# Gated cross-attention in fp32: a setup with fewer, larger DMAs on one queue, block transposes on VectorE, and W_mem's product with chunks outermost

## The chip, the cores and the metric

The kernel runs on one NeuronCore of a Trainium2 chip. The metric is device time in microseconds (us); a profiled execution of the same program gives the trace. Engines are TensorE (PE, with its weight load PEld), VectorE (DVE), ScalarE (ACT), GpSimd (POOL) and SyncE (SP, which here only issues DMAs).

## The reference

`x` is 8 x 1024 x 1024, `memory` (ctx_1024) is 8 x 64 x 512, all in float32.

```python
memory_proj = einsum('bme,de->bmd', memory, W_mem)              # d = 1024, e = 512
scores = einsum('bnd,bmd->bnm', x, memory_proj) / sqrt(1024)
attn = softmax(scores, axis=-1)
memory_context = einsum('bnm,bmd->bnd', attn, memory_proj)
gate = sigmoid(einsum('bnf,df->bnd', concat([x, memory_context]), W_gate) + b_gate)
fused = x + gate * memory_context
return fused * rsqrt(mean(fused**2, -1) + 1e-6) * norm_w
```

## The kernel before, in words

**The main loop.** The rows of x are taken in 16 steps of 512. A step's product of x with the first half of W_gate is a two-level fast matrix product (seven outer products, `outer_product`, each of seven inner ones named kA to kF, where A is used twice); its left operands are sums of x blocks made on VectorE (`outer_s`) and GpSimd (`inner_s`), its right operands are sums of weight blocks, made once in the setup. Scores, softmax and the two small products with the memory's rows (`pc` is the context, the others add the gate's share) are placed between them by slot numbers: `plan(q)` writes down at which slot or beside which product each piece runs. There are 49 slots in a step.

**x and its transposes.** `load_xq` brings 128 rows in as four DMAs, one for each group of 32 partitions, cut so that VectorE's transpose of 32x32 blocks (`transpose_x`) gives the transposed operand `a`. The chunks of the feature axis come out in an order in which a chunk takes 32 columns from each quarter; weights are loaded in the same order (`rows_by_chunk`). `xqpool` has four buffers of 4 KB per partition, so a step's x fills all four.

**The setup.** This is where the change lies. In order:

- `mem` (512 rows of all batches) is loaded in four pieces of 128 rows. TensorE transposes it against an identity (line 165, tiles `pt_mem`), and VectorE copies the result to `memT` (line 171).
- `wm`, W_mem transposed, comes as four chunks of 128 rows; VectorE reorders each to `wmp` (line 179).
- `pm`: for each of the eight output chunks j, the four chunks k of the contraction are accumulated in one PSUM bank. ScalarE and VectorE copy the banks in turn to `mpT` (lines 201 and 203), and pairs of chunks are stored to a DRAM scratch tensor `mpd`, from which a batch's part is read back later as `mpb`.
- `pt_mp`: TensorE transposes mp back into rows (line 211), ScalarE copies it out (line 213), and it is stored to the DRAM scratch `mgd`.
- `pg`: memory rows times the second half of W_gate (`w2`, tiles `w`), in eight banks: four for the first half of the columns and four for the second. The first half of w2's columns is loaded at the start, the second only after the first bank, since the seven buffers of `gpool` hold four. VectorE adds the bias (tile `g`, line 93), and `g` goes to `mgd` too.
- Between pg's banks VectorE works through `w1_tasks`: four outer and 28 inner sums over W_gate's first half, in the tiles `ws` (outer sums 128x2048, inner 128x512). After the seventh bank come the transposes and sums of the first x step (`first`), and GpSimd's `inner_s`.

**Queues.** Loads go through SyncE's queue (`load`), the stores of mpd and mgd through ScalarE's (`scratch`). `pin` keeps program order on each engine and queue. Completion is tracked by eight semaphores, given out in program order over both queues: a DMA is issued only once the one that last had its semaphore has landed. Nearly all matmuls have line 90, tensor operations on two operands line 93, and SyncE's DMAs line 96, as these are helpers.

The waits between engines follow from the tiles: a tile of a pool can be written again only when all readers of its earlier use are done. `mpT` shares its buffers with the left operands `l` of the main loop (tag "l2"), and in the setup pg reads it to the end.

Of the kernel before, what the change touches and what calls it, by code (L numbers as in the profile page):

```python
# [8 lines left out]
F32 = mybir.dt.float32  # L9
# [6 lines left out]
P = 128  # L16
# [4 lines left out]
def tile_gated_cross_attention_rmsnorm(  # L21
# [57 lines left out]
    xqpool = ctx.enter_context(tc.tile_pool(name="xqpool", bufs=4))  # L79
# [15 lines left out]
    def load(o, i):  # L95
        pin(nc.sync.dma_start(o, i))

    def scratch(o, i):
        pin(nc.scalar.dma_start(o, i))

    def t4k(pool, shape, tag, name):
        return pool.tile(shape, F32, tag=tag, name=name)

    def rows_by_chunk(w):

        return w.rearrange("(i j r) f -> i r j f", i=4, r=32)
# [3 lines left out]
    def bank(n, shape, name):  # L110
        return ps.tile(shape, F32, tag=banks[n % 5], name=name)


    memr = mem.rearrange("b m e -> (b m) e").rearrange("(q p) e -> p q e", p=P)
    mem_sb = [t4k(rot, [P, 2, E], "l2", f"mem_sb{i}") for i in range(2)]
    for q in range(NPAIR):
        load(mem_sb[q // 2][:, q % 2, :], memr[:, q, :])
    wm = []
    for k in range(KE):
        t = t4k(xqpool, [P, D], "xq", f"wm{k}")  # L120
        load(t, w_mem_t[k * P : (k + 1) * P, :])
        wm.append(t)
    bias_sb = t4k(small, [P, D], "junk", "bias_sb")
    load(bias_sb, b_gate.partition_broadcast(P))
    w2r = rows_by_chunk(w_gate_t[D:, :])
    w2 = {}

    def load_w2(h):
        for k in range(KD // 2):
            t = t4k(gpool, [P, 2, H], "gate", f"w2_{k}_{h}")  # L130
            for i in range(4):
                load(
                    t[32 * i : 32 * (i + 1), :, :],
                    w2r[i][:, 2 * k : 2 * k + 2, h * H : (h + 1) * H],
                )
            w2[k, h] = t

    load_w2(0)

    w1r = rows_by_chunk(w_gate_t[:D, :])  # L140
    ws = {o: const.tile([P, 7, 2, C], F32, name=f"ws{o}") for o in range(1, 8)}
    R11, R21, R12, R22, T4, T1, T2 = range(7)
    for o, k, h in ((1, 0, 0), (7, 0, 1), (3, 1, 1), (2, 1, 0)):
        for i in range(4):
            for n in range(2):
                load(
                    ws[o][32 * i : 32 * (i + 1), 2 * n : 2 * n + 2, :, :],
                    w1r[i][:, 4 * k : 4 * k + 4, h * H + n * C : h * H + (n + 1) * C],
                )
# [9 lines left out]
    mgd = dram.tile([B, 2, M, D], F32, name="mgd")  # L159
    memT = [t4k(apool, [P, 2, BM], f"a1{i + 1}", f"memT{i}") for i in range(2)]  # L160
    for q in range(NPAIR):
        pt = bank(q, [P, KE, P], f"pt_mem{q}")
        for k in range(KE):
            pin(
                nc.tensor.transpose(
                    pt[:, k, :], mem_sb[q // 2][:, q % 2, k * P : (k + 1) * P], ident
                )
            )
        for i in range(2):
            pin(  # L170
                nc.vector.tensor_copy(
                    memT[i][:, :, q * P : (q + 1) * P], pt[:, 2 * i : 2 * i + 2, :]
                )
            )
    wmp = []
    for k, tag in enumerate(("a21", "a22", "s1", "s2")):
        t = t4k(apool, [P, KD, P], tag, f"wmp{k}")
        pin(
            nc.vector.tensor_copy(
                t.rearrange("p j (i r) -> p j i r", r=32),  # L180
                wm[k].rearrange("p (i j r) -> p j i r", i=4, r=32),
            )
        )
        wmp.append(t)

# [6 lines left out]
    def mp_rows(j, q):  # L192
        return mpT[j // 2][:, j % 2, q * P : (q + 1) * P]

    for j in range(KD):
        pm = bank(j, [P, BM], f"pm{j}")
        for k in range(KE):
            mm(pm, wmp[k][:, j, :], memT[k // 2][:, k % 2, :], k == 0, k == KE - 1)
        dst = mpT[j // 2][:, j % 2, :]
        if j % 2 == 0:  # L200
            pin(nc.scalar.copy(dst, pm))
        else:
            pin(nc.vector.tensor_copy(dst, pm))
            scratch(mpd[:, j - 1 : j + 1, :], mpT[j // 2])

    for q in range(NPAIR):
        stage = t4k(xqpool, [P, D], "xq", f"mp{q}")
        for h in range(2):
            pt = bank(2 * q + h, [P, 4, P], f"pt_mp{q}_{h}")
            for j in range(4):  # L210
                pin(nc.tensor.transpose(pt[:, j, :], mp_rows(4 * h + j, q), ident))
            pin(
                nc.scalar.copy(
                    stage.rearrange("p (i j r) -> p j i r", i=4, r=32)[
                        :, 4 * h : 4 * h + 4, :, :
                    ],
                    pt.rearrange("p j (i r) -> p j i r", r=32),
                )
            )
        for i in range(2):  # L220
            scratch(mgd[2 * q + i, 0], stage[i * M : (i + 1) * M, :])


    def outer_sum(o, a, b):
        tt(nc.vector, ws[o][:, 0:4, :, :], ws[a][:, 0:4, :, :], ws[b][:, 0:4, :, :], ALU.subtract)

    def inner_sums(o):
        w = ws[o]
        for s, a, b in ((T1, R12, R11), (T2, R22, T1), (R12, R22, R12), (T4, R21, T2)):
            yield lambda s=s, a=a, b=b: tt(  # L230
                nc.vector, w[:, s, :, :], w[:, a, :, :], w[:, b, :, :], ALU.subtract
            )
# [6 lines left out]
        lambda: outer_sum(7, 3, 7),  # L239
        lambda: outer_sum(4, 2, 6),  # L240
    ] + [f for o in (6, 7, 5, 4, 2, 3) for f in inner_sums(o)]
# [9 lines left out]
    def load_xq(q, t):  # L251
        b, n0 = where(q, t)
        xq[q, t] = tl = t4k(xqpool, [P, 4, Q4], "xq", f"xq{q}_{t}")
        src = x[b, n0 : n0 + P, :].rearrange("(s c) (i e) -> i c s e", c=32, i=4)
        for i in range(4):
            load(tl[32 * i : 32 * (i + 1), :, :], src[i])

    def transpose_x(q, t, half):

        key = q, t // 2, half  # L260
        if key not in A:
            A[key] = t4k(
                apool, [P, KH, 2 * P], f"a{t // 2 + 1}{half + 1}", f"a{t // 2 + 1}{half + 1}_{q}"
            )
        r = t % 2
        pin(
            nc.vector.transpose(  # L267
                A[key][:, :, r * P : (r + 1) * P].rearrange("p j (s c) -> p s j c", c=32),
                xq[q, t].rearrange("p s (j r) -> p s j r", r=32)[
                    :, :, half * KH : (half + 1) * KH, :  # L270
                ],
            )
        )
# [113 lines left out]
    def load_mg(b):  # L387
        mgs[b] = t4k(small, [P, D], "mg", f"mg{b}")
        load(mgs[b], mgd[b].rearrange("g m d -> (g m) d"))
# [10 lines left out]
    for h in range(2):  # L400
        cols = slice(h * H, (h + 1) * H)
        for q in range(NPAIR):
            pg = bank(n, [P, H], f"pg2_{h}_{q}")
            for k in range(KD):
                mm(pg, mp_rows(k, q), w2[k // 2, h][:, k % 2, :], k == 0, k == KD - 1)
            pool, tag = ((apool, "s4"), (small, "attnT"))[n % 2]
            stage = t4k(pool, [P, H], tag, f"g2_{h}_{q}")
            tt(nc.vector, stage, pg, bias_sb[:, cols], ALU.add)
            for i in range(2):
                scratch(mgd[2 * q + i, 1][:, cols], stage[i * M : (i + 1) * M, :])  # L410
            if n == 0:
                load_w2(1)
                for t in (0, 1, 2, 3):
                    load_xq(0, t)
                load(nw_sb, norm_w.partition_broadcast(P))
            if n < 6:
                while done < len(w1_tasks) * (n + 1) // 6:
                    w1_tasks[done]()
                    done += 1
            elif n == 6:  # L420
                for f in first:
                    f()
                for part in range(2):
                    inner_s(0, 1, part)
            n += 1
# [17 lines left out]
    def plan(q):  # L443
# [17 lines left out]
        if not nxt:  # L461
            for t in range(4):
                at(t0 + 5, load_last, t)
            return
        for i, t in ((2, 0), (3, 1), (4, 2), (5, 3)):
            at(t0 + i, load_xq, q + 1, t)
# [69 lines left out]
    def load_last(t):  # L536
        b, n0 = where(NQ - 1, t)
        xl[t] = t4k(xqpool, [P, D], "xq", f"xl{t}")
        load(xl[t], x[b, n0 : n0 + P, :])
# [36 lines left out]
    def outer_product(q, o, ext):  # L576
# [4 lines left out]
        w = ws[o]  # L581
        kb = {}

        def product(name, tag, lhsT, s, start=True):
            nonlocal slot
            step()
            if name not in kb:
                kb[name] = ps.tile([P, C], F32, tag=banks[tag], name=f"k{name}{q}_{o}")
            for k in range(2):
                mm(kb[name], lhsT[:, k, :], w[:, s, k, :], start and k == 0, k == 1)  # L590
            slot += 1
# [162 lines left out]
```

## Time and profile before

| what | before |
|---|---|
| median of three runs, us | 1013.52 (1008.6, 1013.52, 1014.15) |
| profiled execution, us | 1009.18 |
| its span, us | 1007.4 |
| TensorE busy | 978.7 us, 97% |
| VectorE / ScalarE / GpSimd busy | 75% / 32% / 68% |
| DMA traffic | 126.79 MB, 126 GB/s over the span |
| start of the first kA (end of the setup on TensorE) | 105.83 us |

The profile is of one execution: the span is what the trace covers, and the execution's own time is 1.8 us longer. A matmul in fp32 runs as two passes, so the trace counts two records for each, and records' own lengths overlap; the distance from one start to the next is the price. A row of a timeline has the start, the length, engine, line, operation, output and inputs, how many, and in brackets the idle time before it and what ended that. Groups give busy time and mean ns. A row of stages gives the busy time of each engine, then TensorE's clock (1.00 is full), the DMA engines' share and GB/s.

### The profile page before, as it was taken

How to read it: one execution, taken by the hardware profiler on the slowest of the kernel's cores; microseconds unless marked ns; L12 is line 12 of the kernel's file. 1: busy time of each engine (PE TensorE's matmuls, PEld its weight loads, DVE VectorE, ACT ScalarE, POOL GpSimd, SP SyncE). 2: the span in 40 equal slices, each digit the busy share in tenths (PEclk: the TensorE clock that was granted, in tenths of full speed). 3: DMA queues.
4: the chain of work that ended last, by engine and by line, in shares of the span. 5: the costliest groups of instructions: out<-in, count | busy, mean ns of one | idle time of the engine just before them, and what ended most of it. 6: DMA issues, size and time to landing. Idle time of an engine off the chain costs nothing.

```text
span 1007.4 us, 14639 instructions
## 1 busy us (share of the span) xinstructions
PE 978.7 (97%) x4976; PEld 765.6 (76%) x4976; DVE 760.2 (75%) x1478; ACT 324.7 (32%) x600; POOL 688.0 (68%) x851
## 2 busy tenths in 40 slices
PE   7898999999999999999999999999999999999995
PEld 3443688888878887888888788878888887888883
DVE  2075667878878787878788787878787887878777
ACT  0200023334241523333342415233333424152344
POOL 0000577878878687878788786878787887868772
PEclk9999999999999999999999999999999999999998
DMA  8676508263633727182715546181826363372512
GB/s 255 198 182 180 135 1 178 84 138 97 157 101 84 188 78 164 63 185 87 163 60 130 141 104 158 52 199 63 178 83 137 96 167 97 84 188 89 142 63 84
DMA packets 76522, 126.79 MB, mean 126 GB/s; under 512 B 16288, under 2 KB 53152, under 8 KB 76448
## 3 DMA queue, kind: packets, MB, share of 16 engines
q1 hardware_dynamic: 65312, 88.11, 30.1%
q0 software_dynamic: 8640, 31.46, 17.0%
q10 hardware_dynamic: 2496, 6.29, 2.1%
q8 instruction: 39, 0.64, 0.3%
q14 instruction: 35, 0.29, 0.1%
HBM read 85.98 MB, written 39.85 MB: 125 GB/s over the span
## 4 chain that ended last, share of the span: by engine, by line
PE 79%; DVE 14%; DMA 3%; issue 2%; SPq 1%; ACT 1%; ACTq 0%; POOL 0%; DVEq 0%
PE kA L90 16%; PE pc L90 11%; PE kE L90 9%; PE kF L90 8%; PE kD L90 8%; PE kB L90 8%; PE kC L90 7%; PE psT L90 6%; DVE gate L520 4%; DVE gate L93 3%; PE pm L90 2%; PE pg L90 2%; DVE e L93 2%; DVE u L93 1%; DMA mgd<-g 1%
## 5 line engine op out<-in xcount | busy, mean ns | idle before, releaser
L93 POOL TENSOR_TENSOR gate<-gate,u 128x256 f32<-128x256 f32 x336 | 269.2, 831 | 122.3 <-DVE u L93 100.8
L93 POOL TENSOR_TENSOR l<-a 128x256 f32<-128x256 f32 x128 | 125.6, 981 | 163.3 <-DVE a L267 100.0
L491 ACT ACTIVATE gate<-gate 128x512 f32<-128x512 f32 x128 | 79.1, 629 | 397.7 <-DVE gate L93 397.6
L90 PE MATMUL kA<-ws,a 128*128 128x256 f32 x512 | 131.7, 380 | 0.4 <-ACT u L634 0.4
L90 PE MATMUL pc<-mg,attnT 64*128 64x256 f32 x512 | 127.4, 389 | 0.0
L520 DVE SCALAR_TENSOR_TENSOR gate<-gate,ss,nw_sb 128x512 f32<-128x512 f32 x120 | 116.5, 980 | 1.1
L90 PE MATMUL kC<-ws,l 128*128 128x256 f32 x448 | 115.1, 379 | 0.8 <-DVE g L93 0.8
L90 PE MATMUL kD<-ws,l 128*128 128x256 f32 x448 | 115.0, 379 | 0.0
L90 PE MATMUL kB<-ws,l 128*128 128x256 f32 x448 | 115.0, 379 | 0.0
L90 PE MATMUL kF<-ws,l 128*128 128x256 f32 x448 | 115.0, 379 | 0.0
L90 PEld LDWEIGHTS pc<-mg,attnT 64*128 64x128 f32 x512 | 90.6, 186 | 29.7 <-issue 21.2
L90 PEld LDWEIGHTS kA<-ws,a 128*128 128x128 f32 x512 | 97.0, 190 | 14.7 <-ACT u L634 1.2
L90 PE MATMUL kA<-ws,s 128*128 128x256 f32 x384 | 100.3, 384 | 1.1 <-ACT u L634 1.1
L90 PEld LDWEIGHTS kB<-ws,l 128*128 128x128 f32 x448 | 85.1, 190 | 11.6
L90 PEld LDWEIGHTS kF<-ws,l 128*128 128x128 f32 x448 | 85.1, 190 | 11.6
L90 PEld LDWEIGHTS kC<-ws,l 128*128 128x128 f32 x448 | 83.8, 190 | 11.8 <-POOL l L93 1.1
L90 PEld LDWEIGHTS kD<-ws,l 128*128 128x128 f32 x448 | 83.9, 190 | 10.7
L93 DVE TENSOR_TENSOR gate<-gate,pc 128x512 f32<-128x512 f32 x128 | 87.1, 680 | 5.5 <-ACT gate L491 5.5
L267 DVE STREAM_TRANSPOSE a<-xq 128x512 f32<-128x512 f32 x128 | 86.0, 693 | 0.0
L90 PEld LDWEIGHTS kA<-ws,s 128*128 128x128 f32 x384 | 71.6, 190 | 16.7 <-DVE a L93 6.2
L93 POOL TENSOR_TENSOR l<-s 128x256 f32<-128x256 f32 x96 | 77.9, 811 | 8.0 <-PE kF L90 5.4
L93 DVE TENSOR_TENSOR u<-u,kB 128x256 f32<-128x256 f32 x112 | 46.8, 418 | 46.2 <-PE kB L90 40.2
(94 smaller groups left out, 1695.4 us busy)
## 6 DMA issues: line engine op xcount, KB each, us to landing
xq<-in_x SPq DMA_DIRECT2D x256, 128.0 KB, 5.5
gate<-in_x POOLq DMA_DIRECT2D x60, 512.0 KB, 7.5
out<-gate SPq DMA_DIRECT2D x60, 512.0 KB, 2.6
w<-in_w_gate_t SPq DMA_DIRECT2D x32, 128.0 KB, 3.4
ws<-in_w_gate_t SPq DMA_DIRECT2D x32, 128.0 KB, 3.1
mg<-mgd SPq DMA_DIRECT2D x8, 512.0 KB, 3.6
wm<-in_w_mem_t SPq DMA_DIRECT2D x4, 512.0 KB, 6.4
mgd<-mp ACTq DMA_DIRECT2D x8, 256.0 KB, 4.4
```

What stands on the lines that cost most here:

```text
L90: pin(nc.tensor.matmul(o, lhsT, rhs, start=start, stop=stop, skip_group_check=True))
L93: pin(eng.tensor_tensor(o, a, b, op))
L267: nc.vector.transpose(A[key][:, :, r * P : (r + 1) * P].rearrange("p j (s c) -> p s j c", c=32), xq[q, t].rearrange("p s (j r) -> p s j r" ...
L491: pin(nc.scalar.activation(g, g, AF.Sigmoid))
L520: nc.vector.scalar_tensor_tensor(g[:, cols], g[:, cols], rstd[:, t % 2 : t % 2 + 1], nw_sb[:, cols], ALU.mult, ALU.mult,)
```

## The change

`mem` and `x` are loaded alike: two halves of mem, each in four pieces for 32 partitions, and VectorE's 32x32 transposes give `memT`. W_mem comes in the row order that goes with it, its first chunk between the two halves of mem. The product `pm` has the chunks k outermost and uses eight PSUM banks at once; in the first chunk it takes the first half of mem's rows for all j, then the second. VectorE copies all eight banks, and makes the rows of mp by eight block transposes into `mpq`, which is stored in four DMAs. `w2` is loaded whole, in eight tiles. Both halves of W_gate's first part are loaded in eight DMAs of 512 KB into `w1`; sums go to tiles of their own or in place. Everything is issued on SyncE's queue. x is loaded by four DMAs a step into one buffer of 16 KB per partition, and the last step's second copy of x by one. On TensorE the 48 transposes of the setup are gone and nothing else is added, but pm's first chunk is 16 half-width products in place of eight. SyncE and ScalarE issued 120 DMAs up to the first mg load, SyncE now issues 81.

```diff
-    xqpool = ctx.enter_context(tc.tile_pool(name="xqpool", bufs=4))
+    xqpool = ctx.enter_context(tc.tile_pool(name="xqpool", bufs=1))
-    def scratch(o, i):
-        pin(nc.scalar.dma_start(o, i))
...
+    memq = [t4k(rot, [P, BM // 64, E // 4], "l2", f"memq{i}") for i in range(2)]
+    memr = mem.rearrange("b m e -> (b m) e").rearrange(
+        "(g s c) (i e) -> g i c s e", g=2, c=32, i=4
+    )
+    wm = t4k(xqpool, [P, KE, D], "xq", "wm")
+    wmr = w_mem_t.rearrange("(i j r) d -> i r j d", i=4, r=32)
+    def load_mem(g):
+        for i in range(4):
+            load(memq[g][32 * i : 32 * (i + 1), :, :], memr[g, i])
+    def load_wm(lo, hi):
+        for i in range(4):
+            load(wm[32 * i : 32 * (i + 1), lo:hi, :], wmr[i][:, lo:hi, :])
+    load_mem(0)
+    load_wm(0, 1)
+    load_mem(1)
+    load_wm(1, KE)
+    for k in range(KD):
+        t = t4k(*((gpool, [P, D], "gate") if k < 7 else (apool, [P, D], "s4")), f"w2_{k}")
+        for i in range(4):
+            load(t[32 * i : 32 * (i + 1), :], w2r[i][:, k, :])
+        w2.append(t)
...
-    load_w2(0)
+    w1 = [const.tile([P, 4, D], F32, name=f"w1_{h}") for h in range(2)]
+    for h in range(2):
+        for i in range(4):
+            load(w1[h][32 * i : 32 * (i + 1), :, :], w1r[i][:, 4 * h : 4 * h + 4, :])
...
+    transpose_mem(0, 0)
+    order_wm(0)
+    transpose_mem(1, 0)
+    order_wm(1)
+    transpose_mem(0, 1)
+    transpose_mem(1, 1)
+    order_wm(2)
+    order_wm(3)
...
+    for k in range(KE):
+        for cols in ([slice(0, BM // 2), slice(BM // 2, BM)] if k == 0 else [slice(0, BM)]):
+            for j in range(KD):
+                mm(pm[j][:, cols], wmp[k][:, j, :], memT[k // 2][:, k % 2, cols],
+                   k == 0 and cols.start == 0, k == KE - 1)
     for j in range(KD):
-        pm = bank(j, [P, BM], f"pm{j}")
-        for k in range(KE):
-            mm(pm, wmp[k][:, j, :], memT[k // 2][:, k % 2, :], k == 0, k == KE - 1)
+        pin(nc.vector.tensor_copy(mpT[j // 2][:, j % 2, :], pm[j]))
+    for j in range(0, KD, 2):
+        src = mpT[j // 2]
+        load(mpd[:, j : j + 2, :], src)
+        for g in range(2):
+            pin(nc.vector.transpose(mpq..., src...))
+    for i in range(4):
+        load(mgd[0, :, i * Q4 : (i + 1) * Q4].rearrange("(s c) e -> c s e", c=32),
+             mpq[32 * i : 32 * (i + 1), :, :])
...
-    def load_xq(q, t):
+    def load_xq(q):
+        xq[q] = t4k(xqpool, [P, 16, Q4], "xq", f"xq{q}")
+        src = x[b, n0 : n0 + QT, :].rearrange("(s c) (i e) -> i c s e", c=32, i=4)
         for i in range(4):
-            load(tl[32 * i : 32 * (i + 1), :, :], src[i])
+            load(xq[q][32 * i : 32 * (i + 1), :, :], src[i])
...
-            for i in range(2):
-                scratch(mgd[2 * q + i, 1][:, cols], stage[i * M : (i + 1) * M, :])
+            stage = t4k(small, [P, H], ("mg", "attnT")[n % 2], f"g2_{h}_{q}")
+            load(mgd[1, q * P : (q + 1) * P, cols], stage)
             if n == 0:
-                load_w2(1)
-                for t in (0, 1, 2, 3):
-                    load_xq(0, t)
+                load_xq(0)
                 load(nw_sb, norm_w.partition_broadcast(P))
-            if n < 6:
-                while done < len(w1_tasks) * (n + 1) // 6:
+            if n < 5:
+                while done < len(w1_tasks) * (n + 1) // 5:
-            elif n == 6:
-                for f in first:
+            elif n == 5:
+                for f in first[:6]:
                     f()
                 for part in range(2):
                     inner_s(0, 1, part)
+            elif n == 6:
+                for f in first[6:]:
+                    f()
...
-        for i, t in ((2, 0), (3, 1), (4, 2), (5, 3)):
-            at(t0 + i, load_xq, q + 1, t)
+        at(t0 + 2, load_xq, q + 1)
```

## The prediction

> **What bounds the kernel now.** I read the page first, then busy time by stage, TensorE's timeline through the setup, and at last the queues.
>
> ```profile
> span 1007.4 us, 14639 instructions
> 140.00:250.00 110.00, 109.63 (x589) 89.53 (x588) 85.88 (x173) 39.26 (x72) 84.89 (x105) 1.00 0.48 113
> ```
>
> The second line is a stretch of 110 us of the main loop: TensorE (first pair) is busy 109.63 us at clock 1.00. The loop has no idle time to give back, and its arithmetic is not touched. What the change can win lies ahead of the first product of the loop (kA). TensorE's timeline there (start, length, instructions, idle before and its releaser), with one row of the chain of waits ahead of it:
>
> ```profile
> 12.44 25.17 PE pm L90 x58
> ...
> 41.76 0.66 PE L211 MATMUL pt_mp<-ident,mpT_u 128*128 128x128 f32 x4 [0.86 <-ACT mp L213]
> 44.56 1.99 PE L90 MATMUL pg<-w,mpT_l 128*128 128x512 f32 x2 [2.14 <-ACT mp L213]
> ...
> 79.11 1.98 PE L90 MATMUL pg<-w,mpT_u 128*128 128x512 f32 x4 [1.69 <-DMA w<-in_w_gate_t]
> 83.44 1.96 PE L90 MATMUL pg<-w,mpT_u 128*128 128x512 f32 x4 [2.34 <-DMA w<-in_w_gate_t]
> 92.09 3.60 PE L90 MATMUL pg<-w,mpT_l 128*128 128x512 f32 x8
> 98.96 3.60 PE L90 MATMUL pg<-w,mpT_l 128*128 128x512 f32 x8
> 105.83 1.03 PE L90 MATMUL kA<-ws,a 128*128 128x256 f32 x4
> 108.47 1.10 PE L90 MATMUL kC<-ws,l 128*128 128x256 f32 x4 [0.75 <-DVE g L93]
> ```
>
> The pm products run dense from 12.44 to 37.6. Then transposes of mp, held by ScalarE's evacuations (L213), fill the time to 44.56; the second half of w is waited for twice; kC waits 0.75 for VectorE. One bank of pg takes 98.96 - 92.09 = 6.87 us, that is 0.43 for each of 16 passes. The work that must stay is 64 passes of pm (64 x 0.429 = 27.45) and 8 banks of pg (8 x 6.87 = 54.95): 82.4 us of the 105.83.
>
> **The change part by part.**
>
> *Start.* The first matmul now needs four mem pieces, one transpose on VectorE, wm's first chunk and its copy. SP issues a DMA every 0.46 us (four mem_sb in 1.81), so eight are out at 0.75 + 8 x 0.46 = 4.4 us. The mem pieces now have runs of 512 B. No such row exists; the nearest are x's 1 KB runs, 1636 packets in 107 to 115 us at a DMA share of 0.80 on 16 engines, 63 ns each, and the stretch 97.5 to 101, mostly mpb's 256 B runs, 56 ns a packet. At 55 ns, 64 runs an engine are 3.5 us from the first traffic at about 2.0; wm's 0.5 MB at the 400 GB/s of 6 to 10 us adds 1.3; landing about 1.0; the copy 0.69 (wmp row). Start: 8.5 us. Lower bound: last issue 3.97 + 2.4, the shortest landing of a 128 KB piece, + 0.69: 7.1. Upper: 63 ns a run and the 3.4 us median landing: 10. The remaining 2 MB are not waited for: the second half of mem is needed about 5 us later, the other wm chunks about 9 us later; k outermost hides them.
>
> *Clock.* The PEclk column says 1.00 in the first 12 us, so by it the first products run at full speed. But equal transposes at 4 us and at 38 us differ:
>
> ```profile
> L165 PE MATMUL pt_mem<-ident,mem_sb x16: 272/421/475, 3.7 to 7.2; 128*128 128x128 f32 x16
> L211 PE MATMUL pt_mp<-ident,mpT_l x16: 272/273/273, 37.4 to 40.6; 128*128 128x128 f32 x16
> 45.00:46.00 1.00, 1.00 (x2) 0.34 (x1) 0.00 (x0) 0.00 (x0) 0.00 (x0) 0.50 0.94 253
> ```
>
> (ns min/median/max; then the window with clock 0.50.) [...] This speaks against the change: before, cheap transposes of mem warmed the array; now the first real products do. By the column the cost is 0[...]. The trace has the same event at 44.56: the first 8 passes of pg took 49.79 - 44.56 = 5.23 instead of 3.43. I take this 1.8 (1.5 to 2.1).
>
> *pm to pg.* Removed from TensorE: 16 transposes of mem and 32 of mp, and the wait for ScalarE's eight copies. With k outermost the last round finishes one pm bank each 0.86 us and VectorE copies one in 0.69, so it keeps pace; pg's first product needs only the first copied chunk. The gap 37.6 to 44.56 (7.0) and its cold restart (1.8) go. End of pm: 8.5 + 1.8 + 27.45 = 37.75.
>
> *w2 whole, up front.* No second load after the first bank, so the waits before 79.11 and 83.44 (4.0 shown) go. The 32 pieces (4.2 MB) start at about 11 and are issue-bound at 0.46 each, 15 us, so they land by about 29; at the 1.07 us each of the 16 w pieces at 5.6 to 22.8, the upper bound, the last lands near 46 when 44 is wanted.
>
> *kA.* 37.75 + 54.95 = 92.7 us, against 105.83: 13.1 earlier. VectorE then is at g's last sum when pg ends (before it came 1.8 late), so kC's 0.75 goes too: 13.9.
>
> *VectorE.* Its durations before (busy us, mean ns, then the idle time before and its releasers):
>
> ```profile
> L93 DVE TENSOR_TENSOR ws<-ws 128x512 f32<-128x512 f32 x28 | 17.9, 686 | 0.2
> L93 DVE TENSOR_TENSOR g<-pg,bias_sb 128x512 f32<-128x512 f32 x7 | 4.8, 689 | 27.3 <-PE pg L90 24.3 <-DMA xq<-in_x 3.0
> L93 DVE TENSOR_TENSOR ws<-ws,ws 128x2048 f32<-128x2048 f32 x4 | 9.1, 2290 | 2.9 <-DMA ws<-in_w_gate_t 2.8
> ```
>
> New there: 4 transposes of mem ahead of 37 us, where it idles, and 8 of mp after the copies, 12 x 0.68 = 8.2, and the four pm copies that were ScalarE's (0.69 each); gone are the eight of L171 (0.42 each). From pg's first end (44.6) the five shares of w1 sums cost at most 4.5 + 4 x 0.64 = 7.1 + 0.7 against 6.87 a bank; the x transposes (6 x 0.61) and S sums (3.0 + 1.3) follow one bank earlier than before. All fits, with 5.9 us to spare at the tightest place, below. GpSimd's four ops (0.73 each) wait for pg's last reads of mpT_l (about 87.5) and end at 90.5.
>
> *One queue.* Before, ScalarE's queue carried mpd and mgd:
>
> ```profile
> mgd<-g ACTq DMA_DIRECT2D x16, 128.0 KB, 3.0
> SPq L96 <- DMA mgd<-g: 29.4, 10, 5.0
> SPq L96 <- DMA mpd<-mpT_u: 9.6, 1, 9.6
> ```
>
> SP spent 39 us waiting for these, because the eight completion semaphores are shared by all queues in the order of the program; it loses that and 39 issues (120 setup DMAs become 81). But order now binds. After w1 (served until about 40) come mpd 2 MB, mgd 2 MB in 1 KB runs (8 us, until 53), x's 2 MB (its tile is mpq's, so it waits for mgd, about 55), and behind it the write of the second g. [...] By the row above, 3.0 us, that write is down at 56.5[...] it stands behind 8 us of x and 2 us of nw and lands near 68, while the fourth g, which reuses its stage, is wanted at 65.3. [...] VectorE idles 2.7 us. From there its work to the last g sum is 19.1 us, so up to 73.9 nothing on TensorE moves: cost 0. Last, mpb is issued behind the last g's write, 1.3 us after pg, and needs 3.5 (median) to 5.2; the scores come 7 products later, 6.0 us: 0, at most 0.5.
>
> *Main loop.* x comes in 4 issues a step instead of 16, into one buffer instead of four, so the load starts only after the last transpose:
>
> ```profile
> 188.66 1.30 DVE L267 STREAM_TRANSPOSE a<-xq 128x512 f32<-128x512 f32 x2
> 216.06 11.42 SPq L96 DMA_DIRECT2D xq<-in_x  x16
> 261.37 14.55 SPq L96 DMA_DIRECT2D xq<-in_x  x16
> ```
>
> The last transpose out of the buffer starts at 157.41 and ends at 158.1 in the same timeline, and the first out of the next load is the one at 188.66: 30 us for a load of 11 to 15. No cost. mg's second DMA is one issue per two steps. The tail has the same instructions; its one x load has 36 us. Strides of the weights change, run lengths don't: 0.
>
> **Sum.** 13.9 us from the profiled execution's 1009.18 (span 1007.4 and 1.8 around it): 995.3. That execution is near the fastest of the three timed (1008.6); against their median, 1013.52, it is 999.6. I give 999.5.
>
> **The rivals.**
> - *Writes behind x on the one queue* (0.14). If mgd's 1 KB writes or the broadcast loads are slow (bias landed in 9.2 us), the second g's write lands at 75 to 80, and TensorE waits 1 to 6 us at kA and kC. For: mgd<-g already held SP. Against: 5.9 us of slack. Gain about 10: 1003.5.
> - *Loads pace TensorE as now* (0.13): start at 10, and w2 at 1.07 us a piece costs 2 in the first bank. Gain about 10.5: 1003.
> - *The gain is gone from several such terms together* (0.04): within 5 us of before, about 1010.
> - *Slower: the single x buffer* (0.03). If a load takes longer than the 30 us between its buffer's release and the first transpose, all 15 steps stall. To end over 0.5% slower the stalls must exceed 13.9 + 5 us, 1.3 us a step, so loads of 31.3 us: over twice the 14.55 seen. Then 1019.
> - That the DMAs are not merged or the order not as said is excluded by the instruction order of the two programs.
>
> **How the numbers follow.** The main case (0.66) has 995 to 1005 by the bounds of start, clock and by the scatter of the runs. 0.5% is 5 us, about what a measurement here can tell from no change. Faster by more: 0.66 + 0.14 + 0.13 = 0.93; same 0.04; slower 0.03. The range, 992 to 1007, takes in the two weaker gains and, below, a start at 7.1 with a run like the profiled one.
>
> **What would show it.** Right: first pm at 8 to 9 us with about 3.5 us at half speed (0.86 a pass of 512), no TensorE gap from there to kA at 92 to 94, VectorE waiting for a mgd write before the fourth g, and the rest of the span equal to before's 901.6 from kA. Wrong: an idle row before pg released by w, before kA or kC released by VectorE, before psT by mpb, or a stretch of the loop below 109.6 of 110.

## The result, and the profile after

The changed kernel ran in 1007.0 us (median of six, 1004.26 to 1007.44) against 1011.75 us for the kernel before (six, 1008.6 to 1014.34): ratio 0.9946 (of the means, 1006.2 and 1011.7), 95% interval 0.9919 to 0.9972. The gain in the medians is 4.75 us, where 13.9 were forecast. The profiled execution took 1006.99 us, of which the page's span is 1005.2. The single runs of both kernels lie at two levels (before 1008.6 to 1010 and 1013.5 to 1014.3, after 1004.3 and 1007.0 to 1007.4), and the trace of before is from its lower level, that of after from its upper, so that the two spans differ by 2.2 us only.

The same stretch of the main loop as before, by stage (TensorE's busy time is the first pair):

```profile
140.00:250.00 110.00, 109.63 (x590) 89.82 (x589) 86.74 (x174) 39.23 (x72) 84.86 (x106) 1.00 0.52 115
```

TensorE is again busy 109.63 of 110 us. From the first scores (`psT`) to the end of the span, before needed 1007.4 - 113.03 = 894.4 us and after 1005.2 - 110.98 = 894.2. The loop and the single x buffer cost nothing; whatever was won or lost in these two executions lies ahead of psT. TensorE's timeline there (start, length, instructions, idle before and its releaser):

```profile
8.48 9.82 PE L90 MATMUL pm<-memT,wmp 128*128 128x256 f32 x32 [8.48 <-DVE wmp L190]
18.60 20.87 PE L90 MATMUL pm<-memT,wmp 128*128 128x512 f32 x48 [0.31 <-DVE wmp L190]
39.31 3.60 PE L90 MATMUL pg<-w,mpT_l 128*128 128x512 f32 x8
...
90.81 3.60 PE L90 MATMUL pg<-w,mpT_u 128*128 128x512 f32 x8
95.78 1.13 PE L90 MATMUL kA<-w,a 128*128 128x256 f32 x4 [1.38 <-DVE a L296]
99.42 2.04 PE L90 MATMUL kB<-it,l 128*128 128x256 f32 x4 [2.50 <-POOL l L93]
103.63 2.05 PE L90 MATMUL kC<-w,l 128*128 128x256 f32 x4 [2.17 <-DVE g L93]
105.47 1.91 PE L90 MATMUL kD<-it,l 128*128 128x256 f32 x4
...
110.98 3.67 PE L90 MATMUL psT<-a,mpb 128*64 128x256 f32 x32
```

Up to pg's end the forecast holds to 1.5 us: a start at 8.48 (forecast 8.5), no gap between pm and pg, sixteen dense rows of pg, of which the last ends its work at 90.81 + 3.43 = 94.24 (forecast 92.7). Then three rows wait: kA for VectorE's transpose of x, kB for GpSimd's sum (which needs that transpose), kC for VectorE's last bias sum. From kC's start to kD's are 1.84 us, where the same step takes 0.86 elsewhere. The stage 96 to 108 us says why:

```profile
96.00:108.00 12.00, 7.33 (x18) 5.17 (x18) 8.78 (x15) 0.37 (x1) 5.64 (x8) 0.63 0.41 119
```

The clock was granted at 0.63 on average (PEclk, the third number from the end); in the trace's clock records it is 0.50 from 99.20 to 109.44. The array had waited and ran its next products at half speed. kA at 92.7 and the seven products dense (6.14 us from kA to psT in a run below that doesn't wait) would have put psT at 98.84. It came at 110.98, 12.1 us later: 1.5 from pg's end, 6.05 of waits (1.38 + 2.50 + 2.17), and of the other 4.6 about 4 are the half clock (of its 10.24 us the array worked 8, and half of that is lost); the rest is how the records' ends are counted.

Why VectorE is late is in its own timeline, the idle rows ahead of 96 us:

```profile
57.10 2.29 DVE L93 TENSOR_TENSOR t<-w,t 128x2048 f32<-128x2048 f32 x1 [5.30 <-DMA w<-in_w_gate_t]
...
70.64 0.69 DVE L93 TENSOR_TENSOR g<-pg,bias_sb 128x512 f32<-128x512 f32 x1 [5.19 <-DMA mgd<-g]
...
85.15 0.69 DVE L93 TENSOR_TENSOR g<-pg,bias_sb 128x512 f32<-128x512 f32 x1 [7.88 <-DMA mgd<-g]
...
95.03 3.66 DVE L296 STREAM_TRANSPOSE a<-xq 128x512 f32<-128x512 f32 x6
```

It waits 5.30 us for the second half of `w1`, then twice for a write of g to land, because g has two stages (buffers that hold it until it is written out) and the third and fourth g reuse them: 18.4 us together. The first of these writes stands behind mgd's stores, the second behind x. From 85.15 to 98.6 it has no idle row left and is still behind. SyncE's timeline (start, length from the first issue of a row to the end of the last) shows why the second of those writes is late:

```profile
50.69 7.98 SPq L96 DMA_DIRECT2D mgd<-mpq  x4
58.77 4.26 SPq L96 DMA_DIRECT2D mgd<-g  x1
69.92 2.12 SPq L96 DMA_DIRECT2D xq<-in_x  x4
72.10 0.58 SPq L96 DMA_DIRECT2D nw_sb<-in_norm_w  x1
72.73 31.11 SPq L96 DMA_DIRECT2D mgd<-g  x7
```

x's 2 MB go out at 69.92, when mgd's stores have landed, and the write of g follows at 72.73 and lands at about 85.1: 12.4 us. The forecast had these two points at 55 and 68; that the write waits behind x was the author's estimate there, which no trace of before had shown.

The queue is late because the loads are slow. Stages of before's loads of W_mem and w2, then of after's of w2 and w1 (last two columns: the DMA engines' share, GB/s):

```profile
6.00:10.00 4.00, 2.44 (x11) 1.59 (x11) 3.19 (x8) 0.00 (x0) 0.00 (x0) 1.00 1.02 408
12.00:18.00 6.00, 5.85 (x14) 2.58 (x14) 1.08 (x2) 0.59 (x1) 0.00 (x0) 1.00 1.00 233
```

```profile
18.00:31.00 13.00, 12.69 (x31) 5.62 (x30) 2.94 (x5) 0.00 (x0) 0.00 (x0) 1.00 1.05 235
40.00:48.00 8.00, 8.00 (x20) 3.53 (x19) 6.59 (x11) 0.00 (x0) 0.00 (x0) 1.00 1.02 215
```

All 16 engines count as occupied and move only 215 to 235 GB/s. The trace's landing times give the chain. W_mem's last piece is there at 17.73, w2's last at 35.66 (0.56 us a piece from its first landing on) and w1's at 57.07 (2.5 us for each of its pieces of 512 KB). The 32 issues of w2 took 23.09 us, 0.72 each, since the first of them waited for W_mem's pieces. The stores behind w1 lose nothing more: mpd's and mgd's have landed at 69.91, 12.8 us later, where the forecast had 13.

Three theories followed. *Stage*: the two stages of g, behind x on the one queue, hold VectorE; with more stages the forecast's gain comes. *Partitions*: the loads run at half rate because each DMA touches 32 partitions (235 and 215 GB/s for w2 and w1, where W_mem over 128 had 408). *Clock*: pm's first passes lose 2.8 us at half clock and not 1.8 (9.82 us where full clock would take about 7; the first record of full clock is at 13.87). Against them stands that the loads are simply too much for one queue, or that VectorE has too much work after the transposes have moved to it.

### The profile page after: what moved, and what is told of

It reads as the page before. It is cut to its first block, busy times and chain, and to the rows that moved or that the text cites. A ratio compares the mean times of both kernels' runs of the same rounds, so it can differ in the third digit from the quotient of the medians.

```text
span 1005.2 us, 14277 instructions
## 1 busy us (share of the span) xinstructions
PE 975.3 (97%) x4944; PEld 766.3 (76%) x4944; DVE 766.4 (76%) x1486; ACT 317.6 (32%) x588; POOL 687.3 (68%) x851
## 4 chain that ended last, share of the span: by engine, by line
PE 83%; DVE 13%; issue 1%; DMA 1%; SPq 1%; ACT 0%; POOL 0%; DVEq 0%; ACTq 0%
PE kA L90 17%; PE pc L90 11%; PE kE L90 9%; PE kD L90 8%; PE kF L90 8%; PE kB L90 8%; PE kC L90 7%; PE psT L90 6%; PE pg L90 5%; DVE gate L547 4%; DVE gate L93 3%; PE pm L90 2%; DVE e L93 2%; DVE u L93 1%; DMA wm<-in_w_mem_t 1%
## 5 line engine op out<-in xcount | busy, mean ns | idle before, releaser
L90 PE MATMUL kB<-it,l 128*128 128x256 f32 x448 | 116.0, 382 | 2.5 <-POOL l L93 2.5
L90 PE MATMUL kD<-it,l 128*128 128x256 f32 x448 | 115.9, 381 | 0.0
L90 PE MATMUL kA<-w,a 128*128 128x256 f32 x384 | 99.6, 382 | 1.7 <-DVE a L296 1.4
L90 PEld LDWEIGHTS kB<-it,l 128*128 128x128 f32 x448 | 85.5, 191 | 14.5 <-POOL l L93 2.9
L90 PEld LDWEIGHTS kD<-it,l 128*128 128x128 f32 x448 | 84.5, 191 | 11.0
L90 PEld LDWEIGHTS kA<-w,a 128*128 128x128 f32 x384 | 73.4, 192 | 13.0 <-DVE a L296 2.2
L90 PE MATMUL kE<-it,a 128*128 128x256 f32 x256 | 69.3, 393 | 0.0
L90 PE MATMUL kC<-w,l 128*128 128x256 f32 x256 | 66.7, 384 | 2.2 <-DVE g L93 2.2
L90 PE MATMUL kA<-t,s 128*128 128x256 f32 x256 | 67.4, 386 | 0.0
L90 PE MATMUL kF<-w,l 128*128 128x256 f32 x256 | 65.7, 379 | 0.0
```

Source lines behind the costliest of these rows:

```text
L90: pin(nc.tensor.matmul(o, lhsT, rhs, start=start, stop=stop, skip_group_check=True))
```

## The experiments

**g in stages of its own** (e1). The eight g tiles take turns in five buffers that are idle then, so no bias sum waits for a write; loads and queue stay.

```diff
-            stage = t4k(small, [P, H], ("mg", "attnT")[n % 2], f"g2_{h}_{q}")
+            pool, tag = ((small, "mg"), (small, "attnT"), (apool, "s1"), (apool, "s2"),
+                (apool, "a12"), (small, "mg"), (small, "attnT"), (small, "mg"))[n]
+            stage = t4k(pool, [P, H], tag, f"g2_{h}_{q}")
```

> Only change to the changed kernel: the eight g tiles get five different buffers in place of two, so that VectorE's bias sum does not wait for an earlier g to land in DRAM. Stage theory (VectorE is late at the end of the setup because its g sums wait for writes that stand behind x's load on the one queue, 5.2 + 7.9 us): both waits go, kA starts at about 94.2 us instead of 95.8, kB and kC follow without a gap and at full clock, the scores start at about 100.5 instead of 111.0, and the time falls by about 10 us to some 997 against 1007. Rival, data theory (VectorE is late because the weights and x themselves land late; the waits for g only stand where waits for x would stand): the x transposes before kA then wait for x's load instead, the scores start no earlier than 108, and the time falls by less than 3 us.

Measured: 995.98 us (995.25 to 996.57), ratio 0.9852 (0.9833 to 0.987). TensorE's timeline:

```profile
93.61 1.03 PE L90 MATMUL kA<-w,a 128*128 128x256 f32 x4
94.47 1.03 PE L90 MATMUL kB<-it,l 128*128 128x256 f32 x4
95.34 1.03 PE L90 MATMUL kC<-w,l 128*128 128x256 f32 x4
...
99.75 3.67 PE L90 MATMUL psT<-a,mpb 128*64 128x256 f32 x32
```

and VectorE's waits (in all, times, longest):

```profile
DVE g L93 <- PE pg L90: 7.6, 4, 2.5
...
DVE t L93 <- DMA w<-in_w_gate_t: 3.1, 1, 3.1
```

What was expected came: both waits for a write are gone, and VectorE now waits 7.6 us for TensorE's banks instead of the reverse. That is the forecast's picture with kA 0.9 late, at the forecast's gain: the ratio of the forecast was 999.5/1013.52 = 0.9862. That VectorE has too much work is refuted, as its work is the same here.

**The g writes on ScalarE's queue** (e2): two stages, but nothing ahead of the write.

```diff
-            load(mgd[1, q * P : (q + 1) * P, cols], stage)
+            pin(nc.scalar.dma_start(mgd[1, q * P : (q + 1) * P, cols], stage))
```

> Only change: the eight writes of g to DRAM go on ScalarE's queue, as they did before; all other DMAs stay on SyncE's. Ring-order theory (a write issued after x's 2 MB on the same queue is served after them): the writes land in 3 to 5 us instead of 12, VectorE's two waits of 13.1 us in sum shrink to under 3, and the time falls by 8 to 10 us to about 998. Rival (the sixteen engines are saturated and shared anyway, so which queue issues makes no difference): the writes still take 10 us or more, the scores still start at about 110, and the time stays at 1005 to 1007.

Measured: 999.57 us (998.56 to 1000.36), ratio 0.9887 (0.9868 to 0.9906). Half a hit. The waits of VectorE for mgd<-g are gone, and kA comes at 94.06, but kC waits 2.52 us and psT comes at 103.22. VectorE's waits, then SyncE's:

```profile
DVE a L296 <- DMA xq<-in_x: 8.6, 1, 8.6
```

```profile
SPq L96 <- DMA mgd<-g: 33.4, 3, 16.6
```

Now x is late. SyncE itself stood 33.4 us for writes that ScalarE had issued. For half of it the cause is the completion semaphores, which both queues share: mpd's first store, issued at 39.61 in the changed kernel, goes out at 55.89 here, because it has the same semaphore (102 in the trace) as the first write of g, which lands at 55.81. In the same way mpb waits about 3 us. The remaining 14 us, ahead of mg's load, are at its buffer, which a write of g still reads. The second queue frees the write and holds up the first one.

**Wide loads** (e4). W_mem, w2 and w1 come as DMAs over all 128 partitions with 4 KB runs; two g stages and one queue stay. The rows of these weights are then permuted with respect to memory and x: the kernel does the same work on other rows and does not compute the reference's result.

```diff
-        for i in range(4):
-            load(t[32 * i : 32 * (i + 1), :], w2r[i][:, k, :])
+        load(t, w_gate_t[D + k * P : D + (k + 1) * P, :])
```

> W_mem, w2 and w1 are loaded in DMAs over all 128 partitions, one of 512 KB for each chunk of 128 rows, with the same 4 KB runs and the same bytes. The rows then stand in the order of the weights and not in the order of the transposed x, so the products are with permuted weights. [...] the rate while w2 loads rises from 235 to 380 GB/s or more, as W_mem's load of before had (400), w1's second half is there before 42 us instead of 57.1, x is loaded some 12 us earlier, VectorE is on time and the time falls by 8 to 12 us. Rival, HBM or engine theory (4 KB runs of the weights go at 235 GB/s whatever the partitions): the rate stays below 260 and the time within 2 us.

Measured: 995.68 us (994.47 to 997.28), ratio 0.9849 (0.9825 to 0.9874). The stage of w2:

```profile
18.00:31.00 13.00, 13.00 (x32) 5.78 (x31) 0.00 (x0) 0.00 (x0) 0.00 (x0) 1.00 1.03 411
```

The share is as full as after's 1.05, at 411 GB/s against 235. VectorE no longer waits for w1. It still waits once for a write of g, 6.33 us, and that changes nothing: it then waits 4.4 us for pg's banks, kA comes at 93.16 and psT at 99.29. So the two causes don't add up: with either mended, VectorE's slack covers the other (both together were not run). That one queue is too little is refuted as well; it carried 411 GB/s.

**Order of the pieces** (e3): the four 32-partition pieces of each load go out as 0, 2, 1, 3, so that neighbours in the queue lie 64 partitions apart.

```diff
-        for i in range(4):
+        for i in (0, 2, 1, 3):
```

> Only change: every group of four DMAs over the four groups of 32 partitions in the setup and in x's loads is issued in the order 0, 2, 1, 3 instead of 0, 1, 2, 3. Bytes, pieces, runs and counts are the same. [...] the rate while w2 loads (18 to 31 us) rises from 235 GB/s to 300 or more, w1's second half is there before 50 us instead of 57.1, and the time falls by 4 to 10 us. Rival, engine theory (each of the sixteen engines has a fixed cost for a run or a piece): the rate stays within 10 GB/s of 235 and the time within 2 us of the changed kernel's.

Measured: 997.67 us (995.92, 997.42, 997.91 and 1003.08), ratio 0.9878 (0.9844 to 0.9911); w2's stage at 274 GB/s, short of the 300 expected. Nor is all of this the order's: with the loads and the order as changed, the same stage has 235 (after), 264 (e1), 250 (e2) and 269 GB/s (e11) in different executions. Clearer is the stage of w1 from 36 to 48 us: 244 here, 214 to 223 in those four. VectorE still waited 10.3 us for writes of g, but 0.7 for w1; kC waited 0.39 and psT came at 99.93. The cause of the one run of 1003.08 is open.

**Two queues** (e5): order 0, 2, 1, 3 again, and pieces 2 and 3 on ScalarE's queue, so that both halves of the partitions could be written at once.

```diff
+    def load_i(i, o, a):
+        pin((nc.sync if i < 2 else nc.scalar).dma_start(o, a))
```

> The changed kernel, with the setup's load pieces (mem, W_mem, w2, w1) of partitions 0 to 63 issued on SyncE's queue and those of 64 to 127 on ScalarE's, alternating. The writes and x stay on SyncE's. [...] w2's rate goes to 350 GB/s or more (235 in the changed kernel, 274 with the order 0, 2, 1, 3 on one queue), w1's second half is there before 45 us, and the time comes to about 996. Rival (pieces over 32 partitions are slow in themselves, and the order helped by something else): below 290 GB/s, and 997 to 1003.

Measured: 998.86 us (996.31 to 1001.24), ratio 0.9886 (0.9859 to 0.9913); w2's stage at 252 GB/s, within the scatter just named, and w1's at 276. The 350 expected failed, and the rival's numbers came; its reason does not fit e6, below. VectorE waited 12.0 us for writes of g, and psT 2.12 for mpb. The runs lie in two pairs, at 996.3 and 996.8 and at 1000.9 and 1001.2, and the trace is of the slowest. The two halves on two queues stay at 252 and 276 GB/s, below the 408 of W_mem over 128 partitions in before, and why is open: no run here separates what the two queues do on each DMA engine.

**Which partitions** (e6). Same queue and bytes: w2 as 64-partition pieces over 0 to 63, then over 64 to 127; then w1 over 32 to 95, then over 0 to 31 and 96 to 127. Rows of the weights are permuted as in e4.

```diff
+    for p in (0, 64):
+        for k in range(KD):
+            load(w2[k][p : p + 64, :], w_gate_t[D + k * P + p : D + k * P + p + 64, :])
...
+    for p, m in ((32, 64), (0, 32), (96, 32)):
```

> W_mem, w2 and w1 in the row order of the weights, so the products are with permuted weights. W_mem over 128 partitions; w2 in 64-partition pieces of 256 KB, first all eight pieces of partitions 0 to 63, then all of 64 to 127; w1 first in eight pieces of partitions 32 to 95, then in 32-partition pieces. [...] w2 loads at 220 to 245 GB/s although its pieces have 64 partitions, and w1's pieces over 32 to 95 at 370 or more. Rival (the rate grows with the number of partitions or the size of a piece): both kinds of 64-partition pieces go at one rate, between 280 and 400.

Measured: 1002.72 us in its one run. The stages:

```profile
18.00:31.00 13.00, 13.00 (x32) 5.78 (x31) 0.00 (x0) 0.00 (x0) 0.00 (x0) 1.00 1.04 205
...
34.00:37.00 3.00, 3.00 (x8) 1.33 (x7) 2.50 (x4) 0.00 (x0) 0.00 (x0) 1.00 1.02 406
...
40.00:48.00 8.00, 8.00 (x20) 3.49 (x19) 4.41 (x8) 0.00 (x0) 0.00 (x0) 1.00 1.03 211
```

Partitions 0 to 63, and then 64 to 127, move 205 GB/s, no more than 32 partitions do at the end (211). The 64 partitions that straddle the middle, 32 to 95, move 406, like all 128 in e4. So neither the number of partitions nor the size of a piece decides, but which ones. What makes the 64 in the middle fast and the other two sets slow was not shown.

**A warm array** (e7). Starting from e1: 28 transposes of the identity from 1.4 us on, ahead of pm. Their results are not used.

```diff
+    for i in range(28):
+        pin(nc.tensor.transpose(warm_ps[:, i % 4, :], ident, ident))
```

> The kernel with the g tiles apart, and 28 transposes of the identity on TensorE ahead of the first product, from about 1.3 us on, into a PSUM bank that is overwritten later. Clock theory (the first products run at half clock because the array was idle): the first 32 half-width passes take 6.9 us instead of 9.65, pm ends 2.0 to 2.8 us earlier, and kA starts at 91 to 91.6 instead of 93.6; the time falls by 2 to 2.7 us to about 993.5. Rival, supply theory (those passes are slow because they wait for data or weights, not for the clock): they still take over 9 us and the time does not move.

Measured: 997.63 us (996.44 to 999.35), ratio 0.9875 (0.9858 to 0.9893), no better than e1.

```profile
1.37 6.14 PE L173 MATMUL warm_ps<-ident 128*128 128x128 f32 x28 [1.37 <-POOL ident masks.py:199]
8.21 7.17 PE L90 MATMUL pm<-memT,wmp 128*128 128x256 f32 x32 [0.70 <-DVE wmp L194]
18.81 23.60 PE L90 MATMUL pm<-memT,wmp 128*128 128x512 f32 x48 [3.43 <-DVE wmp L194]
...
97.18 1.03 PE L90 MATMUL kA<-w,a 128*128 128x256 f32 x4
```

```profile
17.00:24.00 7.00, 5.19 (x6) 2.16 (x7) 3.08 (x5) 0.00 (x0) 0.00 (x0) 0.54 1.05 246
```

The first 32 half-width passes took 7.17 us instead of 9.82: the clock had been the 2.65 us, as the theory said. But W_mem's later chunks had not landed, and TensorE waited 3.43 us for them. Behind this wait the clock was 0.54 in 17 to 24 us, and the next 48 passes took 23.60 instead of 20.87. A cold start had been hiding a late load: in the changed kernel too VectorE waits for W_mem's second chunk and has it copied at 18.54 only, so pm could not have gone on before that at any clock. The expected gain did not come. (The trace is of the slowest of the four runs, 999.35.)

**Warm, on two queues** (e8): e7 with 26 transposes and the loads of e5.

> All three that should help together: g tiles apart, the load pieces of partitions 64 to 127 on ScalarE's queue, and 26 transposes of the identity first. [...] the first product starts at about 7 us at full clock and TensorE has no gap up to the scores: kA at 7 + 27.5 + 55 = 89.5 to 91, the time 991 to 993 (0.981 of the kernel before). If the split queues don't speed the start, it is as with the warm array alone, about 993.5.

Measured: 996.18 us (995.11 to 997.82), ratio 0.9861 (0.9842 to 0.9881), level with e1. The transposes ended at 6.1 us and pm began at 8.02: after 1.96 us of idling the stage of 8 to 12 us was granted 0.57.

**The old start** (e9, with e10 and e11 on the same chip). e9 is e1 with before's way of getting mem and W_mem: DMAs of 128 partitions, transposes of mem on TensorE, and pm's first chunk in whole width. k outermost, w2 and w1 stay as changed. e10 is e9 with the order 0, 2, 1, 3 of e3; e11 is e1 once more.

```diff
+    for q in range(NPAIR):
+        load(mem_sb[q // 2][:, q % 2, :], memr[:, q, :])
+    for k in range(KE):
+        load(wm[:, k, :], w_mem_t[k * P : (k + 1) * P, :])
```

> The kernel with the g tiles apart, and with the start of the kernel before: mem and W_mem in DMAs over all 128 partitions and natural rows, mem transposed on TensorE; pm with chunks outermost and all that follows as in the changed kernel. [...] (the new start is slower than the old one, since its 32-partition pieces bring W_mem at 215 to 230 GB/s, and the array is cold): W_mem's last chunk lands before 12.5 us instead of 17.8, the first pm starts at about 9.0 and runs at full speed without a gap, pm ends at 36.5 to 37 instead of 38.7, kA starts at 91.4 to 92 instead of 93.6; the time falls by about 2 us to 994. Rival (the block transposes on VectorE and the finer pieces do help the start, or TensorE's transposes cost what they save): kA at 93.5 or later, the time at 996 or more.

> As the one with the old start, and the groups of 32 partitions of w2, w1, mgd and x in the order 0, 2, 1, 3. VectorE has slack already with the g tiles apart, so by the stage theory this adds nothing that TensorE sees: kA within 0.3 us of the kernel with the old start alone, the time within 1 us of it. If x's faster loads matter in the main loop, it is faster by more than 1 us.

> The kernel with the g tiles apart once more, beside the two with the old start on the same chip: 996 again, about 2 us above the old start [...].

Measured: e9 994.86 us (ratio 0.9849, 0.9816 to 0.9883), e10 994.53 (0.9842, 0.9814 to 0.987), e11 996.11 (0.9855, 0.983 to 0.9879). The medians of e9 and e10 lie 1.3 and 1.6 us below e11's, but the intervals overlap, so a gain over e1 is not shown by them. The single runs lie at two levels: e9 993.65, 993.67, 996.05, 997.05; e10 993.61, 993.63, 995.43, 996.65. The two profiled executions fell on different ones. The weight loads of pm in e9's (993.67 us), then in e10's (996.65 us):

```profile
9.55 0.19 PEld L90 LDWEIGHTS pm<-memT,wmp 128*128 128x128 f32 x1 [0.24 <-issue]
9.98 0.19 PEld L90 LDWEIGHTS pm<-memT,wmp 128*128 128x128 f32 x1 [0.24 <-issue]
```

```profile
10.19 0.34 PEld L90 LDWEIGHTS pm<-memT,wmp 128*128 128x128 f32 x1 [0.52 <-issue]
11.04 0.34 PEld L90 LDWEIGHTS pm<-memT,wmp 128*128 128x128 f32 x1 [0.52 <-issue]
...
14.46 0.34 PEld L90 LDWEIGHTS pm<-memT,wmp 128*128 128x128 f32 x1 [0.52 <-issue]
15.14 0.19 PEld L90 LDWEIGHTS pm<-memT,wmp 128*128 128x128 f32 x1 [0.35 <-issue]
```

One pass each 0.43 us against 0.85 until 15.1: full and half clock, in two kernels whose TensorE work is the same up to here. With it pm takes 27.70 us in e9 and 30.56 in e10, and kA comes at 91.52 and 94.54: 3.0 us apart, as the executions are. The clock column of both stages says 1.00, but this is no reading: the trace's first clock record, the change to full, is at 7.15 us in e9 and at 14.97 in e10, and where there is no record the column shows 1.00. So the sixteen transposes of mem brought full clock in one execution and not in the other. They ended at 7.35 and 7.66 us, and pm began 1.70 and 1.54 us later.

**The gaps filled** (e12): e9 with nine transposes of the identity ahead of mem's transposes and nine behind them.

```diff
+    keep_warm(9)
     for q in range(NPAIR):
...
+    keep_warm(9)
```

> The kernel with the old start of mem and W_mem and the stage of its own for g, and 18 more transposes of the identity, 9 ahead of the transposes of mem and 9 behind them, so that TensorE is at work without a gap from its first instruction to pm's first pass. Theory that the 3 us between executions of one kernel (993.6 and 996 to 997 us for the old start) are pm's first passes at half clock: every execution has a pm of about 27.7 us and kA's products at about 91.5 us, so all of them lie at 993.5 +- 0.5 us and none at 996 to 997. Rival, that the scatter comes from elsewhere (the landing of the loads[...]): the two levels stay, 993.6 and 996 to 997.

Measured: 993.88 us (993.03, 993.77, 993.88, 994.1, 994.46), ratio 0.9818 (0.9792 to 0.9843).

```profile
1.37 2.18 PE L167 MATMUL warm_ps<-ident 128*128 128x128 f32 x9 [1.37 <-POOL ident masks.py:199]
3.38 3.36 PE L174 MATMUL pt_mem<-ident,mem_sb 128*128 128x128 f32 x16
6.58 1.15 PE L167 MATMUL warm_ps<-ident 128*128 128x128 f32 x9
9.18 27.70 PE L90 MATMUL pm<-memT,wmp 128*128 128x512 f32 x64 [1.46 <-DVE wmp L191]
```

None of the five runs lies at the upper level, and the profiled one has the fast pm, with full clock from 5.96 us on. Two, 994.1 and 994.46, are above the 994.0 that was expected at most. Four of the eight runs of e9 and e10 were at the upper level, so five others in a row would come by chance once in 32; and they ran on another chip than those eight. The idea that the array's work ahead of pm decides between the levels is supported, but five runs are no proof. By its median this is the fastest version, and its interval lies below that of the changed kernel (0.9919 to 0.9972); it overlaps those of e1, e4 and e8 to e11. Over e9 it gains 1 us in the median, and nothing over e9's good runs.

## Why the prediction was right in part and wrong in size

**Right.** The bound was read rightly: all of the difference lies ahead of psT, the loop's stretch is unchanged to 0.01 us, and the single x buffer costs nothing. *pm to pg* hit: no gap, and no clock record between the change to full at 13.87 us and the one to half at 99.20. The second load of w2 is gone. *Start* hit (8.48 for 8.5), in part by luck: W_mem's first chunk came 2.36 us behind mem (VectorE's waits end at 5.36 and 7.72), which is 222 GB/s; the forecast had 1.3 us at 400 GB/s and 1.0 for the landing. The *Writes behind x on the one queue* rival named the wait that decided, with its place and its releaser (the stage of g, then kA and kC), and put the whole at 1003.5. Its reason was another: it took mgd's writes or the broadcasts to be slow, but the stores took the 13 us of the main case.

**The step that failed: the pace of the loads in "w2 whole, up front".** It is the one term on which the others hang. It took the loads to be bound by issue at 0.46 us a piece, so that w2 would land by 29, and the chain after it (w1 served by 40, mgd down at 53, x issued at 55, g's write landed at 68) was built on that pace. In fact w2 landed at 35.66, because W_mem's last piece was there at 17.73 only and each piece of w2 took 0.56, and w1 at 57.07, because its 4.2 MB went at about 210 GB/s and not at the 380 that 29 to 40 us asks for. From there on the chain ran as forecast, 15 to 17 us late: x went out at 69.92, and the write of g landed at 85.1. The section had put its upper bound, 1.07 us a piece, against the need of w2 alone, which held, and not against the need of all that queued behind w2. The rate was in the trace of before: 408 GB/s at 6 to 10 us, with W_mem over 128 partitions, and 233 at 12 to 18, with w2 in pieces of 32. The forecast took 400 from the first for a load that the change turns into the second kind. e4 and e6 show that the partitions of a piece make the difference.

**"One queue": the term mis-sized.** It allowed VectorE 2.7 us of waiting, with 5.9 to spare. It waited 5.19 and 7.88 us for writes and 5.30 for w1, 18.4 in all. That the write stands behind x was taken rightly (12.4 us from issue to landing, against a median of 3.0 for before's writes of g on ScalarE's queue), but from an issue 15 us too early; at 85.1 it passed the section's own limit, 73.9, by 11.2 us, and psT came 12.1 late. e1 and e4 bear this out from both ends: with the wait for the stage taken away, or with the loads at full rate, the ratio is close to the forecast's 0.9862 (0.9852 and 0.9849).

**"Clock".** Its size was 1.8 (1.5 to 2.1), an estimate from pg's first eight passes in before (5.23 us for 3.43). The half clock cost pm 2.65 us (9.82 - 7.17, after against e7) to 2.86 us (30.56 - 27.70, e10 against e9); by the clock records it lasted 3.7 to 6.1 us from pm's start on in the eight executions that have no matmul ahead of pm (after 5.4, e5 3.7, e3 6.1), which makes 1.8 to 3.0. The column's 1.00 in the first 12 us, from which the section had its cost of 0, is no reading up to 7.12, the first record in the trace of before. And pm's end does not hang on the clock alone: "the remaining 2 MB are not waited for" failed as well, since W_mem's second chunk, copied at 18.54, held pm at 18.60 whatever the clock. Nor did the forecast or the rival count the second stretch at half clock, from 99.20 to 109.44. This is why the rival's 1003.5 was still too good.

**Sum.** Of the 13.9 us, 1.5 went at pg's end (the clock and W_mem, which overlap), 6.05 to waits at kA, kB and kC, 4.6 mostly to the clock behind them: 12.1. The two traces give 11.85, the 13.9 less the 2.05 us by which psT came earlier than before; the rest is that kC's 0.75 stood for a little over 1 us.

## What to carry to other kernels

Read the DMA rate by stage and by the partitions of each load: a transfer cut into groups of 32 partitions, or into the halves 0 to 63 and 64 to 127, may keep the engines occupied at half the bytes (here 205 to 269 GB/s by stage, in pieces issued in the order of the partitions on one queue, against 406 to 411 for 32 to 95 and for all 128), and everything queued behind it moves. When all transfers share one queue, carry each delay to the last waiter, and give what is written back a buffer of its own rather than a place behind a large load: here five idle buffers moved the ratio from 0.9946 to 0.9852, about 10 us. A matrix engine that waits may pay twice, for the wait and then for its clock: in after 6.05 us of waits brought about 4 more, in e5 psT's wait of 2.12 us brought 1.7 (5.36 us of psT where e1 has 3.67), while in e2, behind a wait of 2.52 us, the clock stayed at 1.00. Such a gap should be priced as a chance of more than its length.

## What the runs showed of the hardware that was not expected

- Which partitions a DMA writes decides its rate: 205 GB/s over 0 to 63 and over 64 to 127, 406 over 32 to 95, 211 over 32 partitions, 411 over 128, always with the engines' share at 1.02 to 1.04. Interleaving the halves on one queue, or giving each its own queue, brought w1's stage from 214 to 223 GB/s to 244 (e3) and 276 (e5), far from 400.
- A DMA on a second queue can hold up the first through a shared completion semaphore: in e2 SyncE waited 16.6 us ahead of mpd for a write of g on ScalarE's queue.
- In the first 5 to 15 us of a program the clock column shows 1.00 because there is no record yet (the first is at 5.96 us in e12 and at 14.97 in e10). The distance of the weight loads, 0.85 against 0.43 us, tells the half clock. Executions that differ in this (e9's and e10's traced ones) lie 3.0 us apart.
- After a change to full clock, a stretch at half clock in the setup lasted 3.41 us (before, e5, e8), 6.83 (e6, e7) or 10.24 (after), that is one, two or three times the same length.
- The length of the idling ahead of pm does not decide by itself: behind 1.46 us in e12 and 1.70 in e9 pm ran at full clock, behind 1.54 in e10 and 1.96 in e8 at half. In e10 the transposes before had not brought full clock at all. Where the limit lies is open.
